# Moving gate and value-row writes to ScalarE's DMA queue and respacing the transfers of a step, in a fused attention and mixture-of-experts layer

## The chip, the cores and the metric

The kernel runs on one core of a Trainium2 chip. TensorE (PE) multiplies matrices, VectorE (DVE), ScalarE (ACT) and GpSimd (POOL) do elementwise work, and SyncE (SP) only issues DMA transfers. SP and ACT each have a queue of their own through which they can start transfers; 16 DMA engines move the data. The engines run side by side, each through its own list of instructions in order, and wait for one another by semaphores.

The metric is the device time of one execution in microseconds (us), the median of several runs. Before the change it is 4316.53 us (three runs, 4314.07 to 4318.04).

## The reference

The input x is (2, 128, 256, 256) in float32. The layer has two halves.

```
# 1. windowed attention on the channel-normalised image, added to x
x = x + conv(ln_c(x))        # qkv = W_qkv . x ; 8x8 windows of queries, 12x12 windows of
                             # keys and values; 4 heads of 32; logits + relative positions
                             # + FIXED_MASK ; softmax ; W_out
# FIXED_MASK is -inf wherever a row or a column of the offset table is even,
# so only every second key row and column of a window takes part.

# 2. eight experts, top two by a softmax router, added to x; a token is a pixel
t = ln_t(tokens(x))
p = softmax(t @ router_w + router_b);  top_p, top_i = top_k(p, 2);  top_p /= sum(top_p)
t = tokens(x) + sum_k top_p[k] * (t @ expert_w[top_i[k]] + expert_b[top_i[k]])
```

## The kernel before

The image is cut into 64 strips of 8 rows of one picture, (128 channels) x (8 x 256 pixels). Because of the mask a strip falls apart into four planes, by odd and even rows and columns, which attend independently. The main loop (line 811) takes one plane n per step: 256 steps, and 7 more that only drain the experts. A step also works ahead and behind: it projects keys, queries and values for plane n+1 (`project`), attends plane n (`scores`, `attend`, `out_project`), takes the norms of two image rows (`norms`), routes two rows of an earlier strip (`route`), and runs the experts for yet earlier rows (`Experts`). The experts of a row pair thus live over three steps: an object is made as `new`, is `nxt` in the next step and `ex` after that.

The experts are not gathered. All eight are computed for every token: for expert e, `times` multiplies the centred tokens `xs` by that expert's gate into `xe[e]`, and `product` adds `ew[e]` times `xe[e]` into one PSUM tile, `acc`. The gate must stand on all 128 partitions with one value per token. It gets there through memory: `route` leaves the gates in a small tile g, `spread` (line 650) transposes it and writes it to a DRAM tile gd with two DMAs (line 661); `fetch` (line 682) reads one expert's row of gd back, repeated over the partitions, into a gate tile `gb` (256 KB); `fetch_means` (line 693) reads the row's mean into `sb`; `fetch_rstd` (line 664) reads the scale for the next attention norm into `rb`, which `ln1` needs.

The values for attention also go through memory. `value_rows` (line 338) projects them, `send_values` (line 363) writes the new rows to a DRAM tile `vrows`, with one DMA, or two where the rows wrap round, and `take_values` (line 373) reads the overlapping windows back into `vwin` with two DMAs.

The order of all work on PE, DVE, ACT, POOL and SP is written out by hand in the loop (`manual_schedule`, line 810); each engine follows the order in which the code emits its instructions. All DMAs of the loop are issued by SP, in that order: gates 5 and 7 of the previous rows, gd (two), vrows (one or two), rb, sb, vwin (two), gates 0, 1, 2, the next strip's piece xt, gate 3, the finished rows to the output, gates 4 and 6.

A `fetch` has a pacer: before its DMA, a given engine writes one column of the gate tile, so that the DMA cannot start before that engine has come to this place. For gates 4, 5 and 7 that is ACT (line 688, a copy), for 0, 1, 2, 3 and 6 it is DVE (line 690, a memset). `load_x` has such a pacer on ACT (line 114). There are eight gate buffers.

TensorE's instruction stream is aligned: line 825 inserts fillers, from step 6 on, so that the code that follows starts 99 instructions before a multiple of 256.

Of the kernel before, what the change touches and what calls it, by code (L numbers as in the profile page):

```python
# [11 lines left out]
F32 = mybir.dt.float32  # L12
# [5 lines left out]
P = 128  # L18
# [33 lines left out]
def kernel(  # L52
# [16 lines left out]
    nc = tc.nc  # L69
# [8 lines left out]
    NT = CH // P  # L78
# [7 lines left out]
    gates = ctx.enter_context(tc.tile_pool(name="gates", bufs=2))  # L86
# [18 lines left out]
    def load_x(i, k, paced=False):  # L105

        if i >= len(strips):
            return
        b, s = strips[i]
        if k == 0:  # L110
            xt[i] = xpool.tile([P, R, W], F32, tag="xt", name=f"xt{i}")
        r = s * R + 2 * k
        if paced:
            nc.scalar.copy(xt[i][:, 2 * k, 0:1], onesm[:, 0:1])
        nc.sync.dma_start(xt[i][:, 2 * k : 2 * k + 2, :], x[b, :, r : r + 2, :])
# [247 lines left out]
    def send_values(n, sent):  # L363

        i, pl = divmod(n, 4)
        for part, vr in sent:
            for k, at, m in runs(i, part):
                nc.sync.dma_start(
                    vrows[pl][1 : PC + 1, at : at + m, :],
                    vr[:, k - part[0] : k - part[0] + m],  # L370
                )

    def take_values(n):

        for half in range(2):
            src = vrows[n % 4][half * HP * 8 : half * HP * 8 + KC].rearrange("c r d -> (c r) d")
            src = src.unsqueeze(1)
            dims = [list(d) for d in src.ap]
            dims[1] = [8 * KR * P, HP]
            nc.sync.dma_start(  # L380
                vwin[n % 2][half * SLOT : half * SLOT + NK],
                bass.AP(src.tensor, src.offset, dims),
            )
# [266 lines left out]
    def spread(f, c, g, nm):  # L650

        gT = small.tile([P, 2, 32], F32, tag="gT", name=f"gT{nm}")
        nc.vector.transpose(
            gT.rearrange("p k i -> p (k i)"), g.rearrange("p k b j -> p (k b j)")
        )
        gd = dram.tile([2 * E * NT, P], F32, tag="gd", name=f"gd{nm}")

        to = gd.rearrange("(k j t) (b i) -> k (t b) j i", k=2, j=E, i=32)
        for k in (1, 0):
            if k or f:  # L660
                nc.sync.dma_start(to[k], gT[:, k])
        return gd

    def fetch_rstd(gd, nm):
# [9 lines left out]
    class Experts:  # L674
# [7 lines left out]
        def fetch(self, e, eng):  # L682


            nm = "_".join(str(v) for v in (*self.at, e))
            self.gb[e] = gates.tile([P, NT * P], F32, tag="gb", name=f"gb{nm}", bufs=8)
            if eng is nc.scalar:
                eng.copy(self.gb[e][:, 0:1], onesm[:, 0:1])
            else:
                eng.memset(self.gb[e][:, 0:1], 0.0)  # L690
            nc.sync.dma_start(self.gb[e], to_all(self.gd, e))  # L691
# [55 lines left out]
    to_store = []  # L747

    def store(i, k):
        b, s = strips[i]  # L750
        r = s * R + 2 * k
        nc.sync.dma_start(out[b, :, r : r + 2, :], xt[i][:, 2 * k : 2 * k + 2, :])  # L752
        if k == R // 2 - 1:
            xt.pop(i)
# [4 lines left out]
    n_planes = 4 * len(strips)  # L759
# [19 lines left out]
    states = {0: {}}  # L779
# [25 lines left out]
    gated, ex, nxt = None, NoExperts(), NoExperts()  # L805
    last = ctile([P, 1], "last")
    pool, dve = nc.gpsimd, nc.vector

    ET = mybir.EngineType
    with tc.manual_schedule(engines={ET.PE, ET.DVE, ET.Activation, ET.Pool, ET.SP}):  # L810
        for n in range(n_planes + 7):
            i, pl = divmod(n, 4)
            score, attn, outp, ahead, norm, rout = none, none, none, none, none, none
# [15 lines left out]
            new, row = NoExperts(), None  # L829
            if gated and gated[0]:  # L830
                rout = route(*gated[0], *gated[2])
            next(rout, None)
            nxt.fetch(5, nc.scalar)
            for _ in rout:
                pass
            next(score, None)
            next(ahead, None)
            nxt.fetch(7, nc.scalar)
            if gated:
                f, c, made = gated  # L840
                gd = spread(f, c, made[0], f"_{n}")
                new = Experts(*f, gd) if f else new
            if n + 1 < n_planes:
                send_values(n + 1, states[n + 1]["sent"])
            if gated and c:
                row = (*c, fetch_rstd(gd, f"_{n}"))
            next(ahead, None)
# [12 lines left out]
            next(norm, None)  # L860
            next(attn, None)
            nxt.means()
            new.fetch_means()
            if n + 1 < n_planes:
                take_values(n + 1)
            for e in (0, 1, 2, 3):
                nxt.times(e, dve)
            new.fetch(0, dve)
            for e in (4, 6):
                nxt.times(e, dve)  # L870
            new.fetch(1, dve)
            ex.end()
            new.fetch(2, dve)
            next(attn, None)
            next(attn, None)


            ex = nxt
            next(norm, None)
            load_x((n + 9) // 4, (n + 9) % 4, paced=True)  # L880
            new.fetch(3, dve)
            while to_store:
                store(*to_store.pop())
            next(ahead, None)
            ex.product(0)
            made = next(norm, None)
            ex.product(1)
            ex.product(2)
            new.fetch(4, nc.scalar)
            nxt.behind(6)  # L890
            nxt.times(5, pool)
            if row:
                ln1(*row, pool)
            if pl == 3 and i + 2 < len(strips):
# [4 lines left out]
            next(outp, None)  # L899
            ex.product(3)  # L900
            next(outp, None)
            new.fetch(6, dve)
            gated, nxt = (f, c, made) if made else None, new
            states.pop(n, None)

# [58 lines left out]
```

## Time and profile before

| | |
|---|---|
| median of the runs | 4316.53 us (4314.07 to 4318.04) |
| the profiled execution's own time | 4331.68 us |
| its span | 4329.9 us |
| mean granted TensorE clock | 0.991 |
| DMA, mean over the span | 236 GB/s |
| busy share of DVE, ACT, POOL | 88%, 30%, 25% |

The profile shows one execution. Times in a timeline are microseconds from the start of the span; a line has the start, the length of the merged stretch, the engine, the source line, the operation, output <- input, and the count. A bracket at the end tells how long the engine was idle before and what ended that. SPq and ACTq are the parts of SP and ACT that issue DMAs. "issue" as a releaser means that the engine waited for nothing that the profile shows. PE is the matmuls, PEld the weight loads. "gb<-gd" and the like are tile names. Where a text here speaks of a time within a step, it counts from the first matmul of line 476, with which a step begins on PE.

Transfers issued in one step in the steady part: 8 gates, 2 vwin, 2 gd, 1 or 2 vrows, and one each of rb, sb, xt and the output. The medians from issue to landing are 5.7 us for gb, 5.1 for vwin, 6.6 for xt, 4.5 for sb, 6.0 for the output, 3.5 for rb, 3.7 to 3.9 for vrows and 3.1 for gd.

### The profile page before, as it was taken

The numbers are of one execution on the slowest core, as the hardware profiler recorded it, in microseconds if no ns is written. First come the engines' busy times: TensorE is split into PE (matmuls) and PEld (weight loads), VectorE is DVE, ScalarE is ACT, GpSimd is POOL, SyncE is SP. The second block draws the span as 40 slices with busy tenths as digits, with TensorE's granted clock in tenths as the row PEclk, the third lists the DMA queues.
The fourth block names the chain that finished last, engine by engine and source line by source line (L and its number), as shares of the span: only waits on it lengthen the run. The fifth ranks groups of instructions, "written<-read, shape, count | busy, mean of one in ns | idle before, by whom it ended". The sixth has DMA issues, their size and how long they took to land. (4 is left out here: it accounts for less than half of the span.)

```text
span 4329.9 us, 224393 instructions
## 1 busy us (share of the span) xinstructions
PE 4220.6 (97%) x94273; PEld 2464.3 (57%) x94273; DVE 3790.8 (88%) x11850; ACT 1320.4 (30%) x3774; POOL 1087.9 (25%) x1126
## 2 busy tenths in 40 slices
PE   7899999999999999999999999999999999999987
PEld 5455555555555555555555555555555555555553
DVE  5798898898888889988889889898888898888877
ACT  3223333332333333233332333333323232333321
POOL 1222222222222222222222222222222222222211
PEclk9999999999999999999999999999999999999999
DMA  4787878788787877878788787887878788787865
GB/s 112 212 245 241 248 236 246 241 244 248 235 239 240 247 236 248 248 235 251 240 247 241 243 247 238 247 248 239 247 233 246 233 250 244 239 246 239 245 190 190
DMA packets 824578, 1022.17 MB, mean 236 GB/s; under 512 B 137634, under 2 KB 409634, under 8 KB 823594
## 3 DMA queue, kind: packets, MB, share of 16 engines
q1 hardware_dynamic: 822864, 1007.52, 76.5%
q8 instruction: 769, 12.60, 1.3%
q14 instruction: 215, 1.76, 0.1%
q10 hardware_dynamic: 730, 0.29, 0.0%
HBM read 863.78 MB, written 143.75 MB: 233 GB/s over the span
## 5 line engine op out<-in xcount | busy, mean ns | idle before, releaser
L716 PE MATMUL acc<-xe,ew 128*128 128x512 f32 x4096 | 1918.4, 601 | 20.7 <-DVE gb L690 14.5
L716 PEld LDWEIGHTS acc<-xe,ew 128*128 128x128 f32 x4096 | 758.4, 190 | 940.3 <-issue 872.7
L707 DVE TENSOR_TENSOR xe<-xs,gb 128x512 f32<-128x512 f32 x1536 | 950.4, 685 | 11.2 <-PE acc L716 1.6
L711 POOL COPY last<-xe 128x1 f32<-128x1 f32 x256 | 47.6, 186 | 3120.0 <-DVE gb L690 3110.9
L707 POOL TENSOR_TENSOR xe<-xs,gb 128x512 f32<-128x512 f32 x512 | 652.1, 1275 | 1.5 <-PE att L524 1.0
L493 PE MATMUL att<-qs,kcol 32*60 32x32 f32 x32768 | 395.3, 223 | 16.7 <-issue 15.9
L493 PEld LDWEIGHTS att<-qs,kcol 32*60 32x60 f32 x32768 | 390.3, 127 | 21.1 <-issue 20.5
L275 POOL TENSOR_TENSOR xn<-xt,rb 128x512 f32<-128x512 f32 x249 | 374.0, 1502 | 93.5 <-DMA rb<-gd 92.7
L524 PEld LDWEIGHTS att<-pT,vwin 64*32 64x32 f32 x32768 | 349.7, 105 | 47.2 <-issue 9.3
L524 PE MATMUL att<-pT,vwin 64*32 64x32 f32 x32768 | 348.4, 200 | 6.5 <-issue 5.5
L501 ACT ACTIVATE pT<-att 128x1024 f32<-128x1024 f32 x256 | 262.2, 1024 | 296.3 <-PE att L493 296.3
L349 PE MATMUL pv<-wt,xn 128*128 128x128 f32 x2048 | 301.9, 291 | 0.9 <-issue 0.9
L412 DVE STREAM_TRANSPOSE uT<-pu 128x512 f32<-128x512 f32 x256 | 183.5, 717 | 132.1 <-PE pu L408 127.2
L576 ACT ACTIVATE sq<-xt 128x512 f32<-128x512 f32 x505 | 292.6, 630 | 0.0
L396 DVE STREAM_TRANSPOSE au<-auT 128x512 f32<-128x512 f32 x256 | 269.7, 1053 | 9.0
L552 PE MATMUL po<-o,wt 128*128 128x512 f32 x512 | 266.4, 602 | 10.2 <-DVE o L544 6.6
L408 PE MATMUL pu<-xn,wrel 128*128 128x512 f32 x512 | 267.5, 604 | 0.9 <-issue 0.9
L433 ACT COPY kcol<-pk 128x560 f32<-128x560 f32 (+2 forms) x344 | 183.4, 533 | 276.5 <-PE pk L422 273.7
L422 PE MATMUL pk<-xn,wt 128*128 128x512 f32 (+2 forms) x528 | 261.9, 580 | 0.0
L447 PE MATMUL pq<-xn,wt 128*128 128x512 f32 x512 | 261.7, 592 | 0.0
L349 PEld LDWEIGHTS pv<-wt,xn 128*128 128x128 f32 x2048 | 252.3, 194 | 11.7 <-issue 1.3
L476 PEld LDWEIGHTS att<-au,keys 32*64 32x64 f32 x8192 | 118.2, 133 | 230.2 <-PE po L552 183.8
(2437 smaller groups left out, 4853.9 us busy)
## 6 DMA issues: line engine op xcount, KB each, us to landing
gb<-gd SPq DMA_DIRECT2D x2048, 256.0 KB, 5.7
vwin<-vrows SPq DMA_DIRECT2D x512, 240.0 KB, 5.1
xt<-in_x_dram SPq DMA_DIRECT2D x256, 256.0 KB, 6.6
sb<-gd SPq DMA_DIRECT2D x256, 256.0 KB, 4.5
out_dram<-xt SPq DMA_DIRECT2D x256, 256.0 KB, 6.0
rb<-gd SPq DMA_DIRECT2D x249, 256.0 KB, 3.5
vrows<-vr SPq DMA_DIRECT2D x168, 256.0 KB, 3.9
vrows<-vr SPq DMA_DIRECT2D x160, 128.0 KB, 3.7
```

Of the source, the lines that this page charges most:

```text
L275: eng.tensor_tensor(xn[i % 2][:, :, :, k, 1 : PC + 1], ln1_src(i, k).rearrange("p (y j x) -> p y x j", y=2, x=2), rb.rearrange("p (y j x) ...
L349: nc.tensor.matmul(pv[:, j * P : (j + 1) * P], lhsT=xp[:, k, 1 : PC + 1], rhs=wv, start=True, stop=True,)
L396: nc.vector.transpose(au.rearrange("p m a s -> p a s m"), auT[n % 2])
L408: nc.tensor.matmul(pu, lhsT=wrel, rhs=inner, start=True, stop=True)
L422: nc.tensor.matmul(pk[:, : m * PC], lhsT=wk, rhs=xp[:, part[0] : part[0] + m, 1 : PC + 1], start=True, stop=True,)
L493: nc.tensor.matmul(sc[rows, h, 32 * t : 32 * t + 32], lhsT=kk[hp, half * HP + t, 0:NK], rhs=qs[hp, m0 : m0 + 2].rearrange("p m a s -> p (m ...
L501: nc.scalar.activation(pT, att[:, :, 0:HQ], AF.Exp)
L524: nc.tensor.matmul(av[hp, half, 32 * t : 32 * t + 32], lhsT=vv[rows, t, hp], rhs=pT[rows, h, 32 * t : 32 * t + 32], start=True, stop=True,)
L552: nc.tensor.matmul(po, lhsT=wo, rhs=state["o"].rearrange("p f z -> p (f z)"), start=True, stop=True)
L576: nc.scalar.activation(sq, src, AF.Square)
L707: eng.tensor_tensor(self.xe[e], self.xs, self.gb.pop(e), ALU.mult)
L716: nc.tensor.matmul(self.acc, lhsT=ew[:, e, :], rhs=self.xe.pop(e), start=(e == 0), stop=not self.xe)
```

## The change

Four things change together. The two gd writes and the vrows writes are issued by ACT instead of SP. The vrows writes are put ahead of the gd writes. The gate tiles have ten buffers instead of eight, and no gate is paced by ACT any more: 5, 7 and 4 move to DVE, 3 moves to POOL. And the transfers take other places in the step: gates 5 and 7 on either side of a part of the routing; then rb, gate 0, xt, gate 1, the first half of vwin, gate 2, the output, gate 3, the second half of vwin, gate 4, sb, gate 6. For that, gate 5's product on POOL and its predecessor `behind(6)` are emitted earlier. The order of the computing instructions on each engine stays as it was, apart from the pacers.

```diff
@@ send_values
-                nc.sync.dma_start(
+                nc.scalar.dma_start(
                     vrows[pl][1 : PC + 1, at : at + m, :],
@@ take_values
-    def take_values(n):
-        for half in range(2):
+    def take_values(n, halves=(0, 1)):
+        for half in halves:
@@ spread
             if k or f:
-                nc.sync.dma_start(to[k], gT[:, k])
+                nc.scalar.dma_start(to[k], gT[:, k])
@@ Experts.fetch
-            self.gb[e] = gates.tile([P, NT * P], F32, tag="gb", name=f"gb{nm}", bufs=8)
+            self.gb[e] = gates.tile([P, NT * P], F32, tag="gb", name=f"gb{nm}", bufs=10)
@@ main loop
             next(rout, None)
-            nxt.fetch(5, nc.scalar)
+            nxt.fetch(5, dve)
+            next(rout, None)
+            nxt.fetch(7, dve)
             for _ in rout:
                 pass
             next(score, None)
             next(ahead, None)
-            nxt.fetch(7, nc.scalar)
+            if n + 1 < n_planes:
+                send_values(n + 1, states[n + 1]["sent"])
             if gated:
                 f, c, made = gated
                 gd = spread(f, c, made[0], f"_{n}")
                 new = Experts(*f, gd) if f else new
-            if n + 1 < n_planes:
-                send_values(n + 1, states[n + 1]["sent"])
             if gated and c:
                 row = (*c, fetch_rstd(gd, f"_{n}"))
@@
             next(norm, None)
             next(attn, None)
             nxt.means()
-            new.fetch_means()
+            nxt.times(0, dve)
+            new.fetch(0, dve)
+            load_x((n + 9) // 4, (n + 9) % 4, paced=True)
+            for e in (1, 2, 3):
+                nxt.times(e, dve)
+            new.fetch(1, dve)
             if n + 1 < n_planes:
-                take_values(n + 1)
-            for e in (0, 1, 2, 3):
-                nxt.times(e, dve)
-            new.fetch(0, dve)
+                take_values(n + 1, (0,))
             for e in (4, 6):
                 nxt.times(e, dve)
-            new.fetch(1, dve)
+            new.fetch(2, dve)
             ex.end()
-            new.fetch(2, dve)
+            while to_store:
+                store(*to_store.pop())
+            nxt.behind(6)
+            nxt.times(5, pool)
+            new.fetch(3, pool)
+            if n + 1 < n_planes:
+                take_values(n + 1, (1,))
             next(attn, None)
+            new.fetch(4, dve)
+            new.fetch_means()
             next(attn, None)
+            new.fetch(6, dve)
 
             ex = nxt
             next(norm, None)
-            load_x((n + 9) // 4, (n + 9) % 4, paced=True)
-            new.fetch(3, dve)
-            while to_store:
-                store(*to_store.pop())
             next(ahead, None)
             ex.product(0)
             made = next(norm, None)
             ex.product(1)
             ex.product(2)
-            new.fetch(4, nc.scalar)
-            nxt.behind(6)
-            nxt.times(5, pool)
             if row:
                 ln1(*row, pool)
@@
             ex.product(3)
             next(outp, None)
-            new.fetch(6, dve)
             gated, nxt = (f, c, made) if made else None, new
```

## The prediction

> **What bounds the kernel now.** I read the page first: engines, slices, DMA queues.
>
> ```profile
> PE 4220.6 (97%) x94273; PEld 2464.3 (57%) x94273; DVE 3790.8 (88%) x11850; ACT 1320.4 (30%) x3774; POOL 1087.9 (25%) x1126
> ...
> q1 hardware_dynamic: 822864, 1007.52, 76.5%
> q8 instruction: 769, 12.60, 1.3%
> ```
>
> TensorE (PE) is busy 97% of the span. Its records, cut where line 476 begins, give 237 steps between 124.9 and 4024.2 us: 137 of them last 16.24 us to within 0.02, and their sum is 3899.3 us, 50.0 over 237 x 16.242. These 50 us, 1.2% of the time, are all that a change of issue can win there. Next I asked for PE's waits in that stretch (us in total, times, longest).
>
> ```profile
> PE att L493 <- issue: 15.7, 30, 1.3
> PE att L524 <- issue: 5.1, 18, 0.7
> PE acc L716 <- issue: 3.8, 10, 0.8
> ```
>
> None of them is a wait for data. The queue named "instruction" brought 769 packets, 12.60 MB: 16.4 kB, or 256 instructions, each. A regular step has 736 weight loads and matmuls, one wait and 31 fillers, 768 instructions, and line 825 pins it so that a block ends after instruction 99. Counted through the code, that is the 18th matmul of line 493, then the fourth weight load of line 716, then the 108th matmul of line 524. The timeline shows the first one:
>
> ```profile
> 3182.65 0.36 PE L493 MATMUL att<-qs,kcol 32*60 32x32 f32 x17
> 3184.36 0.85 PE L493 MATMUL att<-qs,kcol 32*60 32x32 f32 x67 [1.34 <-issue]
> ```
>
> PE stops after 17 matmuls: its next block isn't there. Taken at exactly these three instructions, the excess over the usual spacing is 24.1, 6.9 and 11.4 us in 50, 19 and 37 steps: 42 of the 50 us. I call them boundaries 1 (0.64 us into the step), 2 (6.35) and 3 (10.44). A fetch that follows boundary 3 serves boundary 1 of the next step, one after 1 serves 2, one after 2 serves 3. The packets of the instruction queue start a median 3.1, 1.2 and 2.8 us after boundaries 1, 2 and 3 and last about 1 us; PE stalls once the start is later than about 4.1, 1.75 and 4.3 us.
>
> What makes a fetch late is read from SyncE's (SP) timeline. Here is the step before the stall above (it starts at 3165.71, its boundary 3 is at 3176.15):
>
> ```profile
> 3173.36 0.33 SPq L667 DMA_DIRECT2D rb<-gd  x1
> 3173.78 0.38 SPq L696 DMA_DIRECT2D sb<-gd  x1
> 3174.40 1.42 SPq L380 DMA_DIRECT2D vwin<-vrows  x2
> 3175.93 1.35 SPq L691 DMA_DIRECT2D gb<-gd  x3
> ```
>
> and a quiet one (start 2001.79, boundary 3 at 2012.23):
>
> ```profile
> 2006.02 1.51 SPq L661 DMA_DIRECT2D gd<-gT  x2
> 2007.58 0.58 SPq L368 DMA_DIRECT2D vrows<-vr  x1
> 2009.52 0.33 SPq L667 DMA_DIRECT2D rb<-gd  x1
> 2009.94 1.14 SPq L696 DMA_DIRECT2D sb<-gd  x1
> 2011.18 0.90 SPq L380 DMA_DIRECT2D vwin<-vrows  x2
> 2012.19 1.46 SPq L691 DMA_DIRECT2D gb<-gd  x3
> ```
>
> with, 8.2 to 10.2 us into the step, DMA engines less than half busy (the last numbers are clock, DMA share and GB/s):
>
> ```profile
> 2010.00:2012.00 2.00, 2.00 (x100) 1.10 (x99) 2.00 (x5) 0.00 (x0) 0.00 (x0) 1.00 0.45 141
> ```
>
> Five transfers ahead of the boundary in the first, four in the second, and each nearer to it. Sorting the regular steps by when the second vwin leaves: 0.97 us before boundary 3, the fetch starts 4.0 us after it and the stall is 0.32 us a step; 0.56 before, 3.6 and 0.18; 0.32 before, 3.2 and 0.13; at or after the boundary, 2.5 to 1.9 and 0.05 to 0.01. So the fetch stands behind what was issued up to about 0.35 us before its boundary.
>
> **The change, part by part.** Per step SP issues 17 transfers (18 where vrows goes in two); afterwards ScalarE (ACT) issues 3 or 4 of them and SP 14. No bytes change.
>
> ScalarE's queue. Two gd and one or two vrows issues join it; on SP they take 0.53 to 0.59 us each (1.51 for two in the row above). Three 0.18 us copies (line 688) leave it. The issues fall between the end of vr and kcol:
>
> ```profile
> 2004.90 0.59 ACT L357 COPY vr<-pv 128x512 f32<-128x512 f32 x1
> ...
> 2006.62 0.64 ACT L433 COPY kcol<-pk 128x560 f32<-128x560 f32 x1 [1.04 <-PE pk L422]
> ```
>
> Three issues, 1.7 us, less the 1.04 us idle: kcol, qs, sq and the pacing copy come 0.7 us later, 1.2 us with four. The first to be missed is sq at line 582: ready at 2009.1, read at 2012.5, 3.4 us of cover. Cost 0; with the cover gone, each 0.1 us a step would cost 24 us. A queue holds more than the issue's time, though: by the semaphore numbers in the trace every transfer waits until the eighth before it has landed (SP's waits for landed vwin, 128.1 us, are such). For the first vrows the eighth is the step before's store, issued at 11.0 us and landed 6.0 later (0.8 us into the step); for gd it is gb3 and vwin, down by about 2. Both come before 3.75, so nothing behind them on ScalarE waits.
>
> VectorE and GpSimd. VectorE gets two more memsets of 59 ns (fetches 5, 7 and 4 in, fetch 3 out), GpSimd one; uT waits 0.22 us for PE behind them and GpSimd is busy 25%. Cost 0. With ten buffers, fetch k takes the buffer of ten fetches before, whose reader came earlier on the same engine or a step earlier: no new wait.
>
> SP. The transfers that queued behind the ACT-paced gates (719.7 us of SP waiting on line 688) now go past them. sb leaves at about 13.4 us and is read 6.0 us into the next step, 8.8 us later; it lands in 4.5 us when little is ahead, 6.8 us is the slowest median (xt). vwin, out and xt have a step or more. Cost 0 for all of these as data.
>
> Boundary 2. Before it, gd and vrows go out at 4.2 to 6.3 us; afterwards at 3.75 to 5.6. When vrows left 0.99 us before boundary 2, the fetch began 0.5 us after it; when 0.52 before, 1.5. So the stall there goes from 11.4 to about 1.5: -10 us. Bounds -11 and 0.
>
> Boundary 1. The last issue before it is now gb for expert 6 at about 13.9 us, where before it was that gb at 16.3 with expert 4's at 15.3. In the service sum below the queue clears 1.0 us sooner, so the delay falls from 3.1 to about 2.1, far from 4.1: -6 us. Bounds -7 and 0.
>
> Boundary 3 decides. Service times: landings in a full queue are 0.71 us apart for a 256 KB gate or strip, 1.2 for vwin; from issue to service is 3.47 (rb's landing) less 0.71 and 0.45 for completion, 2.3 us. Check on before, in us of the step: rb 7.7, sb 8.15 and the first vwin 9.93 are issued more than 0.35 ahead of 10.44, and finish at 10.7, 11.4 and 13.4: delay 3.0, seen 2.8. After: vrows leaves ACT at 3.75 and gd behind it at 4.35 (5.0 with two vrows) instead of 4.23 on SP; gd landed 3.25 us after issue behind a gate, I add 0.3 for the slower vrows now ahead of it: 7.5 becomes 7.9 (8.4). Then rb 7.9, gb0 8.3, xt 8.7, gb1 9.25 (after the fourth product of line 707, 9.1), vwin 9.7: five ahead of the boundary, finishing at 10.9, 11.6, 12.3, 13.0 and 14.2. Delay 3.8 us (3.8 for the late gd, since its vwin falls on either side of the cut). Between the groups at 3.6 and 4.0 that is 0.25 us a step, 59 us in 237; the same groups give 29 before. **+30 us.** Bounds: 3.2 us of delay (0.13, +2 us) if service is a little faster; 4.4 us (about 0.45 by extending the groups, +78); and below, no dependence on the queue at all, -29. I take 3.8 because the sum reproduces the quiet and the busy groups.
>
> The Trainium skill speaks on both sides here. "DMA: Bandwidth & Descriptors", section "Queues, rings and completion order", says that each DMA engine goes round between the queues it has work for, packet by packet; by that a fetch waits for one packet and no more, boundary 3 would not care, and with its stalls kept the sum would be -14 us. The groups above (1.9 against 4.0 us) contradict it. "Runtime: NRT & Kernel Launch", "Instruction fetch mechanics", describes refills in 16 KiB blocks, which the 769 packets bear out, and calls them hidden, which the 42 us of stalls don't.
>
> Ends. In the last seven steps without attention, sb leaves sixth after gd instead of first, and the last xs waits for it. The chain at the end has gd landed at 4306.88; six transfers later sb is there at 4306.9 + 2.3 + 6 x 0.71 + 0.45 = 4313.9, and xs (0.65) and six products (0.69 each) lead to 4318.7, where the chain has 4317.87. +1 us, and as much for the steps before: +2, bounds 0 and +6. Start: 0.
>
> Sum: -10 - 6 + 30 + 2 = **+16 us**, 0.38%. The profiled execution took 4331.7 us (span 4329.9), 0.35% above the median 4316.5 of the runs; scaled, 4316.5 x 1.0038 = 4333 us.
>
> **The rivals.** (a) Faster: vwin, slow per byte, makes the delay, not the number ahead. With one vwin ahead of boundary 3 the delay would be that of the groups with the second vwin at or after the boundary, about 2.4 us and 0.05 us a step: 12 us instead of 29, and -17 - 10 - 6 + 2 = -31 us, 4286. For it: vwin's 1.2 us against 0.71. Against: three gates and a strip cost more than one vwin saves. It decides once boundary 3's delay is under 3.6 us (0.18 a step, +14 us, no longer pays for the 16 won elsewhere), which is only 0.2 below my sum; at the extreme all stalls go, -45 us, 4272. (b) Nothing to see: PE stays at 16.24 us, boundary 3 takes back what 1 and 2 give, within 9 us (0.2%, about what this kernel's measurement can tell from no change). (c) ScalarE becomes late. The longest ACT issue at the start of the trace took 1.33 us; four of those, 5.3, less 1.04 and 3.4 of cover, would hold PE at line 582 for 0.9 us a step, +213 us, 4530. From 1.1 us an issue on it decides; the other ACT issues took 0.45 to 0.54.
>
> **How the numbers follow.** Forecast (boundary 3 worse, +9 to +80 us) 0.46; (a) 0.35; (b) 0.13; (c) 0.06. Slower 0.52, same 0.13, faster 0.35. The forecast's own range is 4325 to 4397. Eight in ten: from 4280, which leaves out the far end of (a), to 4380, which leaves out (c) and the upper end of boundary 3.
>
> **What would show it.** In the trace after: PE's waits at L524 and L716 all but gone, those at L493 (17 matmuls, then a gap) about doubled; vrows and gd in ScalarE's queue at 3.7 to 5.6 us of the step, kcol 0.7 us later, line 582 without a wait; SP's rb, gb, xt, gb, vwin within 7.9 to 9.7 us, and the DMA share at 8.2 to 10.2 us of the step up from the quiet step's 0.45. I am wrong if L493's wait shrinks, or if ScalarE holds PE.

## The result and the profile after

The changed kernel takes 4573.11 us (median of four runs, 4564.17 to 4576.09); the kernel before took 4315.3 beside it. The ratio is 1.0588, 95% interval 1.0574 to 1.0602: 5.9% slower. The forecast was 4333, with 4380 as its upper end; the sign was right, the size was not. The two profiled executions have spans of 4329.9 and 4562.4 us, and what follows takes those 232.5 us apart.

The page of the kernel after, its engines and two of its DMA queues (q10 is ScalarE's):

```profile
PE 4273.2 (94%) x94273; PEld 2475.5 (54%) x94273; DVE 3819.3 (84%) x12362; ACT 1245.0 (27%) x3006; POOL 1102.3 (24%) x1382
...
q1 hardware_dynamic: 699024, 931.90, 72.1%
q10 hardware_dynamic: 124570, 75.90, 5.3%
q8 instruction: 769, 12.60, 1.1%
```

The same work and the same bytes, but TensorE is busy for 94% of the span instead of 97%. Its waits in the same 237 steps (126 to 4232 us here; us in total, times, longest) show where:

```profile
PE acc L716 <- issue: 128.3, 190, 1.2
PE att L493 <- issue: 35.8, 67, 2.1
...
PE att L524 <- issue: 6.7, 32, 0.5
```

They are still no waits for data, but the order has turned round: line 716, the smallest before (3.8 us), is now the largest. The timeline of one step:

```profile
3022.47 1.45 PE L716 MATMUL acc<-xe,ew 128*128 128x512 f32 x3
3024.86 2.31 PE L716 MATMUL acc<-xe,ew 128*128 128x512 f32 x5 [0.94 <-issue]
```

TensorE stops after three matmuls, where a block of 256 instructions ends (boundary 2, as the prediction counts them). It stops in the middle of one `product`, of which each makes two matmuls on the same tile, so no operand is late. The packet it waits for follows boundary 1 (3017.6 us) and starts at 3022.4. Taken at the three matmuls, each by its start after the one before it, less the median of that spacing in the kernel before, the steps lose (us in 237 steps):

| stall at | fetch follows | before | after | forecast of the difference | fetch starts after the boundary, before and after |
|---|---|---|---|---|---|
| L493 | boundary 3 | 25 | 53 | +30 | 2.8, 4.1 us |
| L716 | boundary 1 | 7 | 159 | -6 | 3.1, 4.6 us |
| L524 | boundary 2 | 12 | 15 | -10 | 1.2, 2.4 us |

The steps sum up to 4106.0 us instead of 3899.3 (+206.7, of which these three make 183). Most of what lies outside the steps is at the end: from the last time line 476 begins to the end, 107.5 us instead of 90.4.

The queues in the step ahead of that stall (it begins at 2999.5):

```profile
3004.89 1.18 ACTq L661 DMA_DIRECT2D gd<-gT  x2
...
3009.84 0.32 SPq L667 DMA_DIRECT2D rb<-gd  x1
3010.26 0.38 SPq L691 DMA_DIRECT2D gb<-gd  x1
...
3011.70 0.38 SPq L380 DMA_DIRECT2D vwin<-vrows  x1
...
3013.90 1.12 SPq L380 DMA_DIRECT2D vwin<-vrows  x1
...
3015.11 0.60 SPq L691 DMA_DIRECT2D gb<-gd  x1
...
3016.22 0.32 SPq L696 DMA_DIRECT2D sb<-gd  x1
```

rb leaves 10.3 us into the step; the median is 9.7, where it was 7.7 before and forecast at 7.9. SyncE stands from about 2.8 to 9.7 us in waits that gd's landing ends, and then issues twelve transfers, rb among them, into what is left of the step. What SyncE waited for over the whole run (us, times, longest; line 667 is rb, 691 a gate), before and then after:

```profile
SPq L667 <- DMA gd<-gT: 288.0, 243, 2.7
...
SPq L691 <- DMA vwin<-vrows: 128.1, 216, 2.4
...
SPq L691 <- DMA gb<-gd: 78.3, 214, 1.2
```

```profile
SPq L667 <- DMA gd<-gT: 1136.7, 249, 15.5
SPq L667 <- DMA gb<-gd: 315.9, 122, 4.5
SPq L691 <- DMA vwin<-vrows: 274.6, 233, 2.5
SPq L691 <- DMA gb<-gd: 270.3, 475, 2.0
SPq L667 <- DMA sb<-gd: 217.4, 63, 4.9
```

The last four are the rule that a transfer waits until the eighth before it has landed: 1078 us in all. Before, the two lines of that kind come to 206 us.

Four readings went into the first runs. By O, the order and the places of the transfers make the loss: they leave later, and the fetch stands behind them. By Q, ScalarE's queue as such is slower. By F, the stall at line 716 is TensorE waiting for its code; by D, for late data.

After these runs O was put more sharply, as **theory L**: the transfers have become a loop. rb leaves when gd has landed; all others stand in one line behind rb; gate 7 is the last of them, and gd, of the next step, stands behind gate 7. The medians, counted from rb's issue, in us (of the landings that the profile tells):

| kernel | rb landed | gate 7 landed | gd issued | gd landed | next rb (median) |
|---|---|---|---|---|---|
| before | 3.5 | 16.1 | 13.1 | 16.3 | 16.4 |
| after | 3.6 | 16.6 | 12.3 | 17.2 | 17.3 |

The last column is by necessity near the step's length in either kernel, so it doesn't tell what sets the step; how long gd takes does. Before, gd landed 3.2 us after its issue, little more than the least median of this write in any run (2.9): in the 3 us behind its issue the DMA engines moved 178 to 230 GB/s, far from the 350 and more of full stretches, and TensorE's 16.24 us set the step. After, it takes 4.9 us, and behind its issue the engines move 341 to 380 GB/s for 2 us. By theory L the queue is full all the way round, and its 17.3 us are the step. The rival, from then on called **theory F**, has no loop: only what leaves before boundary 1 delays the fetch behind it. By W, a step's transfers need 17.3 us in any order.

### The profile page after: what moved, and what is told of

Its sections match the earlier page's. It is cut to its first block, busy times and chain, and to the rows that moved or that the text cites. A ratio compares the mean times of both kernels' runs of the same rounds, so it can differ in the third digit from the quotient of the medians.

```text
span 4562.4 us, 224325 instructions
## 1 busy us (share of the span) xinstructions
PE 4273.2 (94%) x94273; PEld 2475.5 (54%) x94273; DVE 3819.3 (84%) x12362; ACT 1245.0 (27%) x3006; POOL 1102.3 (24%) x1382
## 4 chain that ended last, share of the span: by engine, by line
PE 87%; issue 6%; DMA 4%; DVE 3%; ACT 0%; SPq 0%; ACTq 0%; DVEq 0%; POOL 0%; POOLq 0%
PE acc L716 37%; PE att L493 7%; PE att L524 6%; PE pv L349 6%; PE plt L582 5%; PE pu L408 5%; PE po L552 5%; PE pk L422 5%; PE pq L447 5%; PE att L476 3%; PE att L514 3%; DMA sb<-gd 2%; DVE xe L707 1%; DMA gb<-gd 1%; DMA xt<-in_x_dram 0%
## 5 line engine op out<-in xcount | busy, mean ns | idle before, releaser
L716 PE MATMUL acc<-xe,ew 128*128 128x512 f32 x4096 | 1951.8, 601 | 161.3 <-issue 132.5
L716 PEld LDWEIGHTS acc<-xe,ew 128*128 128x128 f32 x4096 | 758.4, 190 | 1120.7 <-issue 1042.0
L493 PE MATMUL att<-qs,kcol 32*60 32x32 f32 x32768 | 407.1, 223 | 40.2 <-issue 39.8
L493 PEld LDWEIGHTS att<-qs,kcol 32*60 32x60 f32 x32768 | 396.8, 128 | 49.8 <-issue 47.2
L524 PEld LDWEIGHTS att<-pT,vwin 64*32 64x32 f32 x32768 | 351.5, 105 | 48.5 <-issue 11.5
L524 PE MATMUL att<-pT,vwin 64*32 64x32 f32 x32768 | 349.9, 200 | 8.1 <-issue 7.9
L433 ACT COPY kcol<-pk 128x560 f32<-128x560 f32 (+2 forms) x344 | 183.3, 533 | 615.4 <-DMA vrows<-vr 211.0
L534 DVE STREAM_TRANSPOSE sT<-att 128x512 f32<-128x512 f32 x256 | 182.9, 714 | 114.8 <-PE att L524 111.8
L701 DVE TENSOR_TENSOR xs<-xt,sb 128x512 f32<-128x512 f32 x256 | 174.4, 681 | 107.6 <-DMA sb<-gd 104.4
```

What stands on the lines that cost most here:

```text
L493: nc.tensor.matmul(sc[rows, h, 32 * t : 32 * t + 32], lhsT=kk[hp, half * HP + t, 0:NK], rhs=qs[hp, m0 : m0 + 2].rearrange("p m a s -> p (m ...
L524: nc.tensor.matmul(av[hp, half, 32 * t : 32 * t + 32], lhsT=vv[rows, t, hp], rhs=pT[rows, h, 32 * t : 32 * t + 32], start=True, stop=True,)
L716: nc.tensor.matmul(self.acc, lhsT=ew[:, e, :], rhs=self.xe.pop(e), start=(e == 0), stop=not self.xe)
```

## The experiments

The kernel before ran beside each group of runs, at medians of 4330 to 4335 us, so the ratios are what is to be compared.

### Which part, and is it the fetch

**ScalarE's queue alone**, on the kernel before:

```diff
@@ send_values
-                nc.sync.dma_start(
+                nc.scalar.dma_start(
@@ spread
-                nc.sync.dma_start(to[k], gT[:, k])
+                nc.scalar.dma_start(to[k], gT[:, k])
```

> Only the first part of the change, on the kernel before: the two gd writes and the vrows writes go out by ScalarE, in the old order (gd, then vrows), and everything else stays. Theory O (the order and the places of the transfers make the loss: they are issued later in the step, and TensorE's instruction fetch after boundary 1 stands behind them): gd leaves about as before (4.2 us of the step) and lands by 7.7, so rb stays near 7.7 and the time within 20 us of the kernel before (4295 to 4335). Theory Q (a second queue is what delays gd's landing and the fetch): gd takes over 4.3 us to land instead of 3.2, the fetch after boundary 1 starts 4.5 us late, and 4500 to 4570 us.

4350.64 us, ratio 1.0048 (1.0031 to 1.0065). gd leaves at 3.8 us and lands at 7.5; the fetch after boundary 3 goes from 2.8 to 3.7 us, and L493 from 25 to 46 us. In us it lies above theory O's window, but as a ratio it is a small loss and nowhere near Q's.

**The change without it:**

```diff
@@ send_values
-                nc.scalar.dma_start(
+                nc.sync.dma_start(
@@ spread
-                nc.scalar.dma_start(to[k], gT[:, k])
+                nc.sync.dma_start(to[k], gT[:, k])
```

> The kernel after with that part undone: gd and vrows are issued by SyncE again, in the new order and with all else of the change kept. Theory O: the loss stays, 4530 to 4620 us, with TensorE's stall before the fourth weight load of line 716. Theory Q: most of the loss goes, 4310 to 4350 us.

4577.21 us, 1.0567 (1.0552 to 1.0583). The loss stays; Q has fallen.

**gd ahead of vrows:**

```diff
-            if n + 1 < n_planes:
-                send_values(n + 1, states[n + 1]["sent"])
             if gated:
                 f, c, made = gated
                 gd = spread(f, c, made[0], f"_{n}")
                 new = Experts(*f, gd) if f else new
+            if n + 1 < n_planes:
+                send_values(n + 1, states[n + 1]["sent"])
```

> The kernel after with gd ahead of vrows on ScalarE, as the order was before; all else kept. Theory O with the late gd as its start (rb waits for gd, and every later transfer stands behind rb on SyncE): gd lands about 1 us sooner, rb leaves at 8.7 instead of 9.7 us, the fetch after boundary 1 starts about 0.5 to 1 us sooner, and the time falls by 60 to 180 us, to 4390 to 4510. If the late places of sb and gates 4 and 6 alone matter, gd's place changes little: 4540 to 4580. Theory Q: 4550 to 4580 too.

4486.3 us, 1.0349 (1.0313 to 1.0384): 2.4 points of the 5.9 are vrows' place. rb leaves at 8.5 instead of 9.7.

**The blocks moved by four instructions:**

```diff
-BLOCK, FIRST_LIMIT = 256, 99
+BLOCK, FIRST_LIMIT = 256, 103
```

> The kernel after with TensorE's code moved by four instructions against the blocks of 256 (99 becomes 103), so that boundary 2 comes two matmuls, about 0.85 us, later, and boundaries 1 and 3 by 0.02 to 0.05 us. No data, order or transfer changes. Theory F (the new stall at line 716 is TensorE waiting for its next block of instructions, which starts 4.6 us after boundary 1 where 4.1 would do): the stall has 0.85 us more room, most of its 160 us goes, 4390 to 4460 us. Theory D (the products wait for late data, sb or the scaled tokens): no change, 4550 to 4590 us.

4579.94 us, 1.0571 (1.0555 to 1.0588): no gain, as D expected, but not for D's reason. TensorE's waits in the same steps:

```profile
PE att L524 <- issue: 125.3, 190, 1.2
...
PE acc L716 <- issue: 10.8, 36, 0.9
```

The stall followed the block: at L716 it now comes two matmuls later and falls to 27 us (from 159), while L524 takes 159 (from 15). So TensorE does wait for its code, and D has fallen. The room that boundary 2 gained, 0.85 us, is taken from boundary 3, which hardly moved in the code: the fetch behind boundary 2 has that much less time. So this run alone doesn't say whether both fetches are simply late, or whether the place of a stall is only where a step that is too long for another reason shows itself. The next runs are about that.

### Out of the loop

**The output and xt between gd and rb**, in the kernel after:

```diff
+            while to_store:
+                store(*to_store.pop())
+            load_x((n + 9) // 4, (n + 9) % 4, paced=True)
             if gated and c:
                 row = (*c, fetch_rstd(gd, f"_{n}"))
...
             new.fetch(0, dve)
-            load_x((n + 9) // 4, (n + 9) % 4, paced=True)
...
             ex.end()
-            while to_store:
-                store(*to_store.pop())
...
             states.pop(n, None)
+        while to_store:
+            store(*to_store.pop())
```

> The kernel after with the finished rows' output and the piece xt, which need nothing from gd, issued between gd and rb, where SyncE otherwise stands waiting for gd; all other places kept. Theory L (the step is now as long as a loop of transfers: rb leaves when gd has landed, 3.6 us to rb's landing, then 13 more transfers at 1.0 us each up to gate 7, then vrows and gd, 0.7, and so on round: 17.3): two transfers leave the loop, which then takes 15.3 us, less than TensorE's 16.24, so 4310 to 4400 us. Theory F (only what leaves before boundary 1 delays the fetch behind it, and sb and gates 4 and 6 still leave late): 4530 to 4590. Theory W (the transfers of a step need 17.3 us in all, in any order): 4550 to 4590.

4398.35 us, 1.0148 (1.0123 to 1.0174), just inside L's window. F and W have no place for it: the bytes are the same, and sb and gates 4 and 6 are still the last to leave.

**The same edit with gd ahead of vrows:**

> The same two transfers moved in the kernel with gd ahead of vrows (4486 us). Theory L: vrows is out of the loop as well, 14.5 to 15.5 us for it, and TensorE sets the step: 4300 to 4370 us, below the run with vrows ahead. Theory F and theory W: 4450 to 4500 us.

4348.23 us, 1.0042 (1.0029 to 1.0056). The steps take 3891.8 us, less than the kernel before needs (3899.3); what is lost is the end (102.6 us instead of 90.4).

**The same two moves in the kernel before:**

```diff
+            while to_store:
+                store(*to_store.pop())
+            load_x((n + 9) // 4, (n + 9) % 4, paced=True)
             if gated and c:
                 row = (*c, fetch_rstd(gd, f"_{n}"))
...
             next(norm, None)
-            load_x((n + 9) // 4, (n + 9) % 4, paced=True)
             new.fetch(3, dve)
-            while to_store:
-                store(*to_store.pop())
...
             states.pop(n, None)
+        while to_store:
+            store(*to_store.pop())
```

> The same two transfers moved in the kernel before, all else as before. Theory L: its loop takes 16.1 to 16.4 us, as long as TensorE's 16.24, so it has no slack; with two transfers out it gets 1.3 us or more, part of the 50 us of fetch stalls goes, and the time is 10 to 40 us below the kernel before. Against: xt and the output are then served just ahead of boundary 3, whose stalls grow, 0 to 40 us above it.

4416.28 us, 1.0206 (1.0154 to 1.0258): a miss for L, which saw no slack in this kernel's loop. Where the loop is not the limit, the two transfers only stand ahead of boundary 3. rb lands 4.7 instead of 3.5 us after its issue, the fetch after boundary 3 starts at 4.0 instead of 2.8 us, and L493 loses 89 us. The groups by which the prediction was made (0.32 us a step at a start of 4.0) give 76.

**Without the transfer of gate 7** (expert 7 is multiplied by gate 6's values):

```diff
+            if e == 7:
+                self.gb[7] = self.gb[6]
+                return
             nm = "_".join(str(v) for v in (*self.at, e))
```

> The kernel after without the transfer of gate 7 (expert 7 is multiplied by gate 6's values, so the experts' sum is another). Gate 7 leaves 1.8 us after boundary 1. Theory L: one transfer less in the loop, 0.9 us a step, 16.4 us, 4340 to 4400. Theory F: nothing that leaves before boundary 1 is gone, so the fetch behind it is as late as it was: 4520 to 4580.

4475.25 us, 1.0323 (1.0308 to 1.0339). Neither. By theory F nothing would come of it, and 2.6 points did: gd lands at 8.4 instead of 9.7 us. But only 0.3 us a step came of the 0.9 that L promised. Now gate 5 leaves 9.9 us behind rb instead of 9.2, and it lands no sooner (16.0 instead of 15.8). SyncE's waits at a gate for a pacer on VectorE rose from 55 to 183 us between 200 and 4000 us; that the pacers, which keep TensorE's time, begin to hold the transfers as the loop gets shorter would fit, but no run shows it by itself. A transfer is not worth its service time by a fixed price.

### The other parts

**vrows ahead of gd in the old order**, on the run with ScalarE's queue alone:

```diff
+            if n + 1 < n_planes:
+                send_values(n + 1, states[n + 1]["sent"])
             if gated:
                 f, c, made = gated
                 gd = spread(f, c, made[0], f"_{n}")
                 new = Experts(*f, gd) if f else new
-            if n + 1 < n_planes:
-                send_values(n + 1, states[n + 1]["sent"])
```

> The kernel before with gd and vrows on ScalarE (4351 us) and vrows ahead of gd, nothing else. Theory L: vrows' 0.4 to 0.9 us enter the loop from rb to rb, which stands at 16.4 us without them; the step becomes 16.8 to 17.2 us, 4430 to 4560 us. Theory of the prediction (gd lands 0.3 us later, boundary 3's fetch a little later): 4360 to 4400.

4386.93 us, 1.0128 (1.0101 to 1.0154), 0.8 points above the run without it. Too little for L, in the range of the prediction's way of reckoning: rb leaves at 8.5 instead of 7.5 us, the fetch after boundary 3 starts 4.2 us after it instead of 3.7, and L493 loses 82 us instead of 46, where the steps lose 22 in all.

**Pacers and ten buffers in the old order**, on that same run:

```diff
-            self.gb[e] = gates.tile([P, NT * P], F32, tag="gb", name=f"gb{nm}", bufs=8)
+            self.gb[e] = gates.tile([P, NT * P], F32, tag="gb", name=f"gb{nm}", bufs=10)
...
-            nxt.fetch(5, nc.scalar)
+            nxt.fetch(5, dve)
+            next(rout, None)
+            nxt.fetch(7, dve)
...
-            nxt.fetch(7, nc.scalar)
...
-            new.fetch(3, dve)
+            new.fetch(3, pool)
...
-            new.fetch(4, nc.scalar)
+            new.fetch(4, dve)
```

> The kernel before with gd and vrows on ScalarE (4351 us) plus the new pacers and the ten gate buffers (gates 5, 7 and 4 by VectorE, 3 by GpSimd; 7 earlier), while SyncE's order of the other transfers stays the old one. If the new order of SyncE's transfers is what costs the 135 us between 4351 and 4486, this stays within 30 us of 4351. If gate 7's earlier place is (it then stands ahead of gd in a full queue), 4400 to 4490.

4336.52 us, 1.0011 (0.9997 to 1.0025). They cost nothing. So the new order of SyncE's transfers (with gate 5's product emitted earlier) makes the whole step from 1.0011 to 1.0349.

**sb back behind rb in the last seven steps**, in the kernel of 4348 us:

```diff
             nxt.means()
+            if n >= n_planes:
+                new.fetch_means()
...
-            new.fetch_means()
+            if n < n_planes:
+                new.fetch_means()
```

> The kernel with gd first and the output and xt ahead of rb (4348 us); in the last seven steps, without attention, sb leaves right behind rb as in the kernel before. From the start of the last step with attention to the end that kernel needs 102.6 us, the kernel before 90.4. If sb's late place costs it: 89 to 93 us, and 4330 to 4345 us in all. If the new pacers do: 100 us and more, 4345 to 4355.

4333.17 us, 1.0005 (0.9989 to 1.002). The end takes 89.2 us, not 102.6. The last waits of xs for sb are the difference: 3.6 us here from 4240 us on, 16.0 in the kernel of 4348 us. In the kernel after, from 4454 us on, they were (us, times, longest)

```profile
DVE xs L701 <- DMA sb<-gd: 20.1, 6, 9.0
```

**The output alone moved**, in the kernel after:

```diff
+            while to_store:
+                store(*to_store.pop())
             if gated and c:
                 row = (*c, fetch_rstd(gd, f"_{n}"))
...
             ex.end()
-            while to_store:
-                store(*to_store.pop())
...
             states.pop(n, None)
+        while to_store:
+            store(*to_store.pop())
```

> The kernel after with the output alone moved ahead of gd and rb (the run with both moved took 4398 us). The output then leaves at about 2.8 us, behind gate 7 and ahead of gd. Theory L: it is still in the loop that ends with gd, which doesn't shorten: 4540 to 4590 us; it is xt, issued behind gd, that shortened it. Theory F (only what leaves before boundary 1 and late delays the fetch): the output no longer stands ahead of boundary 1, and 4400 to 4480 us.

4599.15 us, 1.0616 (1.059 to 1.0642), a little slower even than L's window and far from F's. The output now leaves at 3.3 us, behind gate 7 and ahead of gd. It no longer stands ahead of boundary 1, and the fetch there starts as late as ever (4.8 us), because rb has gone from 9.7 to 10.5. F, as put before the run, has fallen.

### Which transfer

**xt alone moved behind gd**, in the kernel after:

```diff
+            load_x((n + 9) // 4, (n + 9) % 4, paced=True)
             if gated and c:
                 row = (*c, fetch_rstd(gd, f"_{n}"))
...
             new.fetch(0, dve)
-            load_x((n + 9) // 4, (n + 9) % 4, paced=True)
```

> The kernel after (4573 us) with xt alone issued between gd and rb; the output stays in its new place behind gate 2. Theory L: xt leaves the loop, 0.9 us a step, and little of the 1.07 us of excess is left: 4350 to 4410 us, the same gain as with both moved. If moving xt and the output together was needed: 4450 to 4550.

4474.87 us, 1.0328 (1.0299 to 1.0357): 2.6 points, half of what L expected, though alone the output gives nothing and with xt it gives 1.8 more. Again the effects don't add.

The next three are on the kernel with gd ahead of vrows (1.0349). **sb right behind rb:**

```diff
             nxt.means()
+            new.fetch_means()
...
             new.fetch(4, dve)
-            new.fetch_means()
```

> The kernel with gd ahead of vrows (4486 us) with sb issued right behind rb, as before the change. Theory L: sb is in the loop at either place, so 4460 to 4490, less some 15 us at the end of the kernel, where the last steps no longer wait for sb: 4455 to 4480. If sb's late place is what costs the 150 us of the new order: 4330 to 4390.

4667.85 us, 1.0778 (1.0744 to 1.0812): worse than any. Neither window had it. The granted clock was lower here, 0.978 to 0.982 in its four runs for 0.984 to 0.993 in all others; if that took its share of the time, it would be about one of the 4.3 points above the run without this edit. **Both vwin right behind rb:**

```diff
             nxt.means()
+            if n + 1 < n_planes:
+                take_values(n + 1)
...
             new.fetch(1, dve)
-            if n + 1 < n_planes:
-                take_values(n + 1, (0,))
...
             new.fetch(3, pool)
-            if n + 1 < n_planes:
-                take_values(n + 1, (1,))
```

> The kernel with gd ahead of vrows (4486 us) with both vwin transfers right behind rb, as before the change, and sb late. Theory L, by which the order within the loop doesn't matter: 4470 to 4500. If vwin split up among the gates is what costs (the same eleven transfers behind rb took 11.6 us in the new order and 10.8 in the old one): 4350 to 4420.

4337.41 us, 1.0011 (0.9995 to 1.0027). All but 0.1 of the 3.5 points are gone, with one transfer pair moved inside the loop. **Both edits together:**

> Both: rb, sb, vwin, vwin, then gates 0, xt, 1, 2, the output, 3, 4, 6; of the new order only the earlier xt, output and gates 3 and 4 are left. Theory L: 4455 to 4490. If the front of the order is what costs, near the 4337 us of the kernel with the old order: 4330 to 4370. In between, the rest is the earlier xt and output.

4400.72 us, 1.0155 (1.0121 to 1.0188).

That the order within the loop doesn't matter, as L had it, is refuted twice. The loop itself stays, and the medians of these kernels say what the order does to it (us from rb's issue; the last column is how long gd takes to land):

| kernel | rb landed | gate 7 landed | gd landed | gd's landing less its issue |
|---|---|---|---|---|
| gd first | 3.4 | 16.8 | 16.9 | 4.6 |
| gd first, sb in front | 3.4 | 17.7 | 17.9 | 5.0 |
| gd first, both in front | 3.6 | 16.5 | 16.6 | 2.7 |
| gd first, vwin in front | 3.7 | 16.1 | 16.3 | 3.1 |

The same 13 transfers behind rb take 13.4, 14.3, 12.9 and 12.4 us from rb's landing to gate 7's. With 12.4, gd lands about as soon as before the change and the steps' median is TensorE's 16.24 us; with 13.4 it doesn't, and the median is 16.93. With both in front gd lands quickly too, but rb, sb, both vwin and a gate leave ahead of boundary 3, and L493 loses 94 us.

### The cause in the kernel after, and a faster one

**The kernel after with vwin alone put back**, by the same edit as in the run with vwin in front:

> The kernel after (4573 us) with only this undone: both vwin transfers are issued right behind rb again; vrows stays ahead of gd on ScalarE, and sb, xt, the output and the gates stay where the change put them. Theory V (vwin split up among the gates is what makes the loss): 4360 to 4420 us, that is some 50 to 90 for vrows ahead of gd and for the end on top of the kernel before. If vrows ahead of gd keeps the loop longer than TensorE's step by itself: 4450 to 4520.

4389.78 us, 1.0116 (1.0093 to 1.0139), as theory V expected. SyncE's queue in one step:

```profile
3028.07 0.32 SPq L667 DMA_DIRECT2D rb<-gd  x1
3028.50 0.90 SPq L380 DMA_DIRECT2D vwin<-vrows  x2
3029.50 0.39 SPq L691 DMA_DIRECT2D gb<-gd  x1
```

The issue lines of the page (size, median us to landing), after and then with vwin put back:

```profile
vwin<-vrows SPq DMA_DIRECT2D x512, 240.0 KB, 7.6
...
vrows<-vr ACTq DMA_DIRECT2D x168, 256.0 KB, 5.5
...
gd<-gT ACTq DMA_DIRECT2D x516, 16.0 KB, 4.6
```

```profile
vwin<-vrows SPq DMA_DIRECT2D x512, 240.0 KB, 5.1
...
vrows<-vr ACTq DMA_DIRECT2D x168, 256.0 KB, 3.2
...
gd<-gT ACTq DMA_DIRECT2D x516, 16.0 KB, 2.9
```

From rb's landing to gate 7's it is 11.4 us instead of 13.0, gd's landing falls from 4.6 to 2.9, and the stall at L716 from 159 to 8 us. What is left is L493 (76 us, the fetch after boundary 3 at 4.3 us) and the end (106.1 us), the two places where the prediction had seen a loss. The two halves of vwin were moved together; no run says which of them it was.

**gd first, vwin in front, and sb in front in the last seven steps**, three edits that were shown above:

> The kernel with gd first and both vwin transfers right behind rb (4337 us, steady part 3888.7 us against 3899.3 of the kernel before), and sb right behind rb in the last seven steps, which took 13 us off a kernel's end before. If the two add up: 4318 to 4328 us, 0.1 to 0.35% below the kernel before. If the end hides it: 4333 to 4340.

4320.31 us, 0.9972 (0.996 to 0.9984): below the kernel before by 0.3%, and, by the two ratios, below the kernel after by 5.8%. The page's engines, and TensorE's waits in the 237 steps:

```profile
PE 4220.1 (98%) x94273; PEld 2467.1 (57%) x94273; DVE 3789.4 (88%) x12362; ACT 1246.1 (29%) x3006; POOL 1095.4 (25%) x1382
```

```profile
PE att L493 <- issue: 9.2, 19, 1.2
...
PE att L524 <- issue: 1.7, 10, 0.2
...
PE acc L716 <- issue: 1.4, 5, 0.6
```

The steps take 3882.9 us instead of 3899.3, and the end 89.7 instead of 90.4. So ScalarE's queue, ten buffers, the pacers and the earlier xt and output are together a small gain, once gd goes first and vwin isn't late.

## Why the prediction was wrong

**Boundary 3: the number came, in part by luck.** +30 us was forecast at L493 for a delay of 3.8 us; the trace has +28 for 4.1. That it was the fetch, held up by what stood in the queue, and that the sign was slower, was right, and alone with ScalarE's queue, with xt and the output in the kernel before, and with vrows ahead of gd, the stall grew with the fetch's start about as the groups had it. But the terms were others. The sum had five transfers ahead of the boundary, a vwin among them; rb left so late that in 217 of 237 steps two to four had left by 0.35 us before it, and no vwin. The sum had them 0.71 us apart; rb, gate 0, xt and gate 1 landed 1.1 to 1.4 us apart (medians 3.6, 4.9, 6.0 and 7.4 us behind rb's issue). And by the groups a delay of 4.1 us would have cost over 76 us in all, not 53.

**Boundary 1: the step that failed.** "In the service sum below the queue clears 1.0 us sooner, so the delay falls from 3.1 to about 2.1, far from 4.1: -6 us." It cleared later: the delay is 4.6 us and L716 loses 159 us instead of 7, which is 152 of the 207 us that the steps lost. Gate 6, the last issue before the boundary, left at 17.1 us of the step, not 13.9, and landed 7.4 us into the next one instead of 5.5 before. Of the 3.2 us by which it left later than forecast, 1.8 are rb's late start; the rest came between rb and gate 6. The sum ran once, from rb to boundary 3, with a queue that was empty at its start, as it was in the quiet step before. It was never carried round into the next step, where what it leaves over stands ahead of gates 5 and 7, of vrows and of gd, and so of the next rb. How much slack the loop had before, no run shows: the 16.4 us from rb to rb are the step itself, and two runs for which theory L had taken them as the loop's own length, xt and the output moved in the kernel before and vrows ahead of gd in the old order, missed its windows.

**gd's landing** is where the loop closes. 7.9 us was forecast (0.3 added for vrows), 9.6 measured. gd was issued nearly as said (4.6 us, the second at 5.4, for 4.35 and 5.0), but took 4.4 to 4.8 us where 3.25 + 0.3 was put. With gd ahead of vrows, 2.4 points of the loss go; in the old order the same swap costs 0.8. So the price of a place in the queue is not a fixed one.

**vwin's place** was costed at 0 ("vwin, out and xt have a step or more") as data, and the stalls are indeed no waits for data. Put back in the kernel after, it returns 4.7 of the 5.9 points. The prediction used that vwin takes 1.2 us of service for a gate's 0.71, and only for the transfers ahead of boundary 3.

**"Every transfer waits until the eighth before it has landed ... nothing waits"**: wrong. In the kernel after, the eighth before the second gd is mostly the second vwin, which lands 5.0 us into the step, not "by about 2"; SyncE's waits of the kind rose from 206 to 1078 us, and on ScalarE kcol stood idle 615.4 us in all instead of 276.5, 211.0 of them ended by the landing of vrows. It is not shown how much of the loss goes through this rule, since no run changed it.

**Boundary 2** was to gain 10 us and lost 3: gd and vrows leave nearly when they were to leave, but the queue ahead of them is not empty (gate 7 lands about 9 us into the step). **The end** was to cost 2 us, at most 6, and cost 17; sb's late place was named, but one wait was counted where six came to 20.1 us. **ScalarE's queue** was rightly put at nothing for the arithmetic: line 582 lost 4 us in all, and rival (c) did not come.

**The rivals.** (a), fewer transfers of vwin ahead of boundary 3, hence faster, has the right transfer and the wrong sign: taken away from the front, vwin slowed all that came behind. The prediction weighed the page "DMA: Bandwidth & Descriptors" of the Trainium skill (section "Queues, rings and completion order"), which has each DMA engine go round between the queues packet by packet. The prediction took from it that a fetch would wait for one packet; a fetch that starts 4.6 us after its boundary doesn't fit that reading. The range went to 4380 because boundary 3 alone, at its worst, was to cost 78 us; no rival had the transfers themselves as the bound, though the table of queues had them at 76.5% of the time.

**What stays open.** Why vwin late in the line makes the same 13 transfers 1 to 1.6 us longer, and why sb in front makes them 0.9 us longer still when vwin is late. The profile says where the time is lost: averaged over the steps, 10 to 11.5 us behind rb, the engines move 237 GB/s in the kernel after, at a DMA share of 1.12, and 367 with vwin put back, at 1.01. With vwin put back the slow stretch is an earlier one: 159 GB/s from 1 to 3 us behind rb, where the kernel after moves 197, at shares of about 0.7. In a single step the stretches look like this, 9.3 to 11.3 us and 8.6 to 10.6 us behind their rb (start and end, busy times, clock, DMA share, which can pass 1 where packets overlap, and GB/s), first after, then with vwin put back:

```profile
3142.12:3144.12 2.00, 2.00 (x63) 1.72 (x52) 1.77 (x9) 1.36 (x2) 0.00 (x0) 1.00 1.13 257
```

```profile
3036.70:3038.70 2.00, 1.97 (x158) 1.83 (x139) 1.85 (x9) 0.33 (x2) 0.00 (x0) 1.00 1.05 399
```

In the first, the second vwin is on its way: it was issued at 3137.2 and lands at 3145.4. Its 512-byte packets take a median 27 ns and a gate's 2048 bytes 84, so they are slower per byte; that they slow what is served beside them would fit, but no run measures it by itself.

## What to carry to other kernels

Follow a chain of transfers round until it meets itself: if the first of a step waits for a landing, and that landing stands behind the last of the step before, the whole line is a loop, and its length has to be compared with the step of the busiest engine. The time from one round to the next can't show that, since it is the step in any case; how long the transfer that closes the loop takes to land, against its least, can. Where the loop is the limit, what helped here was to issue what needs nothing from it while the queue's head waits, the short write that closes it ahead of the long ones, and vwin, the slow transfers, right behind the head. In the kernel before, where the loop was not the limit, the first of these moves cost 2 points. Where a stall shows says little: shift it, as the block's place does, see whether the time follows, and ask which neighbour paid for the room.

## What the runs showed of the hardware

- A fetch of TensorE's next 256 instructions (16 KB) started a median 3.1, 1.2 and 2.8 us after the three boundaries of a step before, and 4.6, 2.4 and 4.1 after, with no change to TensorE's code; with 0.85 us of room moved from one boundary to the one before, the stall changed places and the time stayed (4580 us against 4573).
- One pair of transfers, moved a few places in its queue, was worth 4.7 points (ratio 1.0588 to 1.0116), with no byte, no operand and no engine's work changed.
- The effects of moving transfers did not add: the output alone +0.3 points, xt alone -2.6, both -4.4.
- In the kernel with gd first, the issue right behind rb on SyncE took a median 1.05 us, in the kernel after 0.37, for the same gate 0. Nothing here explains it.
